# A graph-attention and mixture-of-experts kernel on one core: the middle of a step in another order, and a prologue that the planner orders

## The chip, the cores and the metric

The kernel runs on one core of a Trainium2 chip. A core has several engines, each of which works through its own list of instructions: TensorE (PE, matrix products; PEld in the tables is its loading of weights), VectorE (DVE), ScalarE (ACT), GpSimd (POOL) and SyncE (SP, which here only issues transfers). Engines wait for each other by semaphores. The metric is device time in microseconds (us) of one execution.

## The reference

There are 128 graphs of 64 nodes with 256 features each (8192 rows, float32), an adjacency matrix for each graph, and two layers. A layer is a graph attention over each graph's 64 nodes and then a mixture of experts in which each row takes the two best of eight experts; both are residual and both work on the layer norm of x.

```python
# layer 0 (layer 1 has a leaky ReLU on e, another gate, hidden 512, ReLU)
x = x + gnn(layernorm(x), adj)
x = x + ffn(layernorm(x))          # layer 0: ffn adds its tokens too

def gnn(h, adj):                   # h: 128 x 64 x 256
    Wh = h @ W
    e = (Wh @ a1)[:, :, None] + (Wh @ a2)[:, None, :]
    attention = softmax(where(adj > 0, e, -9e15), axis=-1)
    return elu(attention @ Wh)

def moe(tokens):                   # tokens: 8192 x 256
    logits = tokens @ router       # 8 experts
    w, e = top_k(logits, 2); w = softmax(w)
    return sum over both choices of w * (act(tokens @ w1[e] + b1[e]) @ w2[e] + b2[e])
```

Hidden size is 256 with GELU in layer 0 and 512 with ReLU in layer 1.

## The kernel before

**Blocks.** The rows of a layer are cut into 16 blocks of 512 rows (4 tiles of 128), so that there are 32 blocks in all. Each block has two Python generators, which are advanced stage by stage, so that the stages of several blocks can be woven together by hand.

`attend` (called through `a(i)`, one stage a call) does the attention of block i: layer-norm statistics on DVE, their reciprocal root on POOL (rs_g, L232) and the mask (cap_g, L279, POOL); the bias nb_g (L238, DVE) and the normalised xn_g (L240, ACT); the transposes pt_g on PE and their copies xt_g (L255 on DVE, L257 on ACT); the product pw_g with the weights (L290); sm_g (L301, DVE); the scores pe_g on PE (L309, L310) and ee_g, the masked exponentials; **a stage of two DVE instructions, the reciprocal of the sums and the normalising of ee_g (L334, L335)**; **a stage in which PE transposes ee_g into pp_g (L339) and pp_g is copied to pT_bd, one half by DVE (L341), the other by ACT (L342)**; the product po_g of pT_bd with wh_g (L348, PE) and its exponential ex_g (L356, ACT); and the sum xb_g (L362, L365, DVE).

`route` (called through `r(i)`) does the gating of block i: its layer norm (rs_r, nb_r, tn_r), the transposes pt_r, the logits pl_r (PE, L419) with the copy lg_r (L428) and a first search for the largest (L372 to L383, five DVE instructions); **the second search (L445 to L450: the best one masked, the five instructions again, and mm and q; eight small DVE instructions)**; the weights of the two choices; pn_r on PE (L476, L477), from which positions in the experts' lists follow (at_r, ps_r, ix_r, L479 to L494, DVE); eight indirect scatters of the rows into the lists in DRAM (L499, POOL); and a plan of which full groups of rows can be worked off.

**Slots.** Rows that are routed to one expert are worked off in slots of 256. SP fetches a slot's rows (xg_s, L688) and its expert's weights (wc_s, L740, L744, L748). Then `x()` transposes them (px_s on PE, L771, copy xT_s on DVE, L775), `h()` is the first product (ph_s, L853) with the activation on ACT (L862), and `y()` the second (py_s, L884) with the bias added on DVE (ys_s, L891). In layer 0 POOL scatters ys into res (L900); in layer 1 ACT weights it (L926) and POOL scatters it with accumulation into the output (L929).

**What sets the order.** The prologue starts three blocks' chains (and parts of blocks 3 and 4), woven by a list of calls (`chains`). Then the main loop runs one step for each t from FIRST = 3 to 31: it issues the attention of block n = t + 1, the routing of block t and t - 1 and the slots in an order written out by hand. `tc.manual_schedule(engines=ORDERED)`, entered before the first constant, holds four engines to the written order:

```python
ORDERED = {SP, mybir.EngineType.PE, mybir.EngineType.DVE, mybir.EngineType.Activation}
```

POOL is never held: a planner places its instructions, as it would on the other engines without this statement. The planner places by its own estimate of when operands are ready; each engine still runs what it was given in order. PSUM limits what can be in flight: the attention's tiles share two buffers (tag "a"), the routing's two (tag "r"), and px_s has one, ph_s two, py_s one.

Of the kernel before, what the change touches and what calls it, by code (L numbers as in the profile page):

```python
# [14 lines left out]
ORDERED = {SP, mybir.EngineType.PE, mybir.EngineType.DVE, mybir.EngineType.Activation}  # L15
# [20 lines left out]
def adj_ffn_kernel(  # L36
# [78 lines left out]
        return int(b >= CUT)  # L115

    ctx.enter_context(tc.manual_schedule(engines=ORDERED))
    ident = const.tile([P, P], F32, name="ident")  # L120
    make_identity(nc, ident)
    imod = const.tile([P, NG], F32, name="imod")
# [272 lines left out]
    def unordered(group, ins, keep=()):  # L395

        tc.declare_no_dep(
            ins.ins, group=group, keep=[i.ins for i in keep], reason="different rows"
        )
        tc.add_to_no_dep_group(group, ins.ins)  # L400
# [294 lines left out]
    class Slots:  # L695
# [140 lines left out]
        def h(self):  # L836
            k = self.nh
            self.weighted()
            if k == self.nx or k == self.ny + 2:
                return  # L840
            self.nh += 1
            sl = self.all[k]
            l = sl["l"]
            wc, xT = sl["wc"], sl["xT"]
            hT = slot.tile([P, HC[l], SL], F32, tag="hT", name=f"hT_s{k}")
            for f in range(0, HC[l], 2):
                ph = ps_s.tile([P, 2, SL], F32, tag="ph", name=f"ph_s{k}_{f}", bufs=2)
                cols = [slice(r.start * P, r.stop * P) for _, r in sl["of"]]
                for j in range(2):
                    for w, r in zip(wc, cols):  # L850
                        for c in range(KD):
                            o = c * HC[l] * P + (f + j) * P
                            nc.tensor.matmul(  # L853
                                ph[:, j, r],
                                lhsT=w[:, o : o + P],
                                rhs=xT[:, c, r],
                                start=(c == 0),
                                stop=(c == KD - 1),
                            )
                for j in range(2):  # L860
                    for w, r in zip(wc, cols):
                        nc.scalar.activation(  # L862
                            hT[:, f + j, r], ph[:, j, r], AF.Gelu if l == 0 else AF.Relu,
                            bias=w[:, OB1[l] + f + j : OB1[l] + f + j + 1],
                        )
            sl["hT"] = hT
            if l == 1 and sl["rest"]:
                self.spare(k)

        def y(self):  # L870
            k = self.ny
            self.weighted()
            if k == self.nh:
                return
            self.ny += 1
            sl = self.all[k]
            l = sl["l"]
            wc, hT = sl["wc"], sl["hT"]
            py = ps_s.tile([P, ST, D], F32, tag="py", name=f"py_s{k}")
            ys = slot.tile([P, ST, D], F32, tag="ys", name=f"ys_s{k}", bufs=4)  # L880
            for w, (_, r) in zip(wc, sl["of"]):
                for t in range(r.start, r.stop):
                    for f in range(HC[l]):
                        nc.tensor.matmul(  # L884
                            py[:, t, :],
                            lhsT=hT[:, f, t * P : (t + 1) * P],
                            rhs=w[:, O2[l] + f * D : O2[l] + (f + 1) * D],
                            start=(f == 0),
                            stop=(f == HC[l] - 1),
                        )  # L890
                nc.vector.tensor_tensor(  # L891
                    ys[:, r, :],
                    py[:, r, :],
                    w[:, OB2[l] : OB1[l]].unsqueeze(1).to_broadcast([P, r.stop - r.start, D]),
                    ALU.add,
                )
            sl["ys"] = ys
            for t in range(sl["st"]):
                if l == 0:
                    ins = nc.gpsimd.indirect_dma_start(  # L900
                        out=res[sl["part"]],
                        out_offset=self.row(sl, t),
                        in_=ys[:, t, :],
                        in_offset=None,
                        bounds_check=2 * N - 1,
                        oob_is_err=False,
                    )
                    unordered(f"res{sl['part']}", ins)
            if l == 1:
                self.ready = k  # L910
            self.ahead()
# [59 lines left out]
    def there(i):  # L971
        return 0 <= i < len(blks) and blks[i]

    def load(i, first=None):
        if there(i):
            k = blks[i]
            if k["l"]:
                assert all(s["l"] or s["part"] != part(k["b"]) for s in slots.all[slots.ny :])
            k["in"] = load_block(k["l"], k["b"], first)
            k["a"] = attend(k["l"], k["b"], k)  # L980

    def a(i, n=1):
        if there(i):
            for _ in range(n):
                next(blks[i]["a"], None)

    def r(i, n=1):
        if there(i):
            k = blks[i]
            if "r" not in k:  # L990
                k["r"] = route(k["l"], k["b"], k)
            for _ in range(n):
                next(k["r"], None)
# [49 lines left out]
    r(2, 2)  # L1043
    slots.fetch()
    slots.ahead()
    for t in range(FIRST, len(blks)):
        n = t + 1
        more = slots.nf - slots.ny > SB or len(slots.all) - slots.ny > SB
        if t + 3 != NB:
            load(t + 3)  # L1050
        a(n)
        h()
        x()
        a(n)
        r(t - 1)
        a(n)
        h()
        r(t)
        slots.fetch()
        if more:  # L1060
            x()
        a(n)
        r(t)
        early = n < len(blks) and blks[n]["l"] == 1
        if t + 2 != NB:
            a(t + 2)
        if early:
            a(n)
        y()
        r(t - 1)  # L1070
        if t + 2 != NB:
            a(t + 2)
        if not early:
            a(n)
        (h if more else x)()
        r(t)
        a(n)
        y()
        r(t - 1)
        a(t + 2, 1 + 2 * (t + 2 == NB))  # L1080
        if more:
            x()
        a(n)
        r(t)
        x()
        h()
        r(t - 1)
        a(n)
        if more:
            y()  # L1090
        x()
        r(t - 1)
        a(n)
        h()
        r(n)
        y()
        a(t + 2)
        r(t - 1)
        r(t)
        r(t)  # L1100
        y()
        slots.fetch()
        x()
        r(n)
        r(t)
        if t + 3 == NB:
            load(t + 3)
# [58 lines left out]
```

## Time and profile before

| what | value |
|---|---|
| median of 3 runs | 1396.14 us (1396.05 to 1398.04) |
| profiled execution | 1397.4 us, of which the span is 1395.6 us |
| instructions in the profile | 22284 |
| busy share of PE / PEld / DVE / ACT / POOL | 87% / 74% / 63% / 46% / 53% |
| mean granted clock of PE | 0.952 |
| matmuls of the slots, py_s L884 and ph_s L853 | 393.7 and 385.7 us |
| attention po_g L348 | 74.2 us busy, PE idle ahead of it 29.8 us |
| second half of pT_bd, L342 on ACT | 11.7 us busy |
| scatters of rows into the lists, L499 on POOL | 248.7 us, 256 instructions |
| scatters of ys, L929 and L900 on POOL | 213.0 and 144.5 us |
| first list fetch by SP, first px_s | 119.83 and 122.57 us after the span's start |

The profile shows one execution; times in it are microseconds from the span's start. A granted clock of 1.00 is PE's full speed. "Idle before, releaser" is the time in which an engine stood still just before an instruction and the event that ended the wait. A row of a list is one instruction or several equal ones in sequence, with the count at the end. The prologue lies in the first 120 us, the steps of layer 0 up to some 500 us, those of layer 1 up to some 1160 us, and the last slots after that.

### The profile page before, as it was taken

What the parts mean: (1) busy time and instruction counts of PE and PEld (TensorE: products, weight loads), DVE (VectorE), ACT (ScalarE), POOL (GpSimd) and SP (SyncE); (2) the same over time, 40 slices, a digit from 0 to 9 for tenths busy, and PEclk for the clock granted to TensorE, in tenths of its full rate; (3) what the DMA queues carried; (4) which work ended last, traced back from release to release, by engine and by line L of the source; (5) the groups of instructions that cost most, each with busy time, mean ns of one, the idle gap of its engine ahead of it and who ended that gap; (6) DMA issues with size and microseconds to landing.
All of it is one profiled execution on the core that took longest, in us unless ns stands there. A gap on an engine that the chain in (4) does not pass through costs nothing. (4 is left out here: it accounts for less than half of the span.)

```text
span 1395.6 us, 22284 instructions
## 1 busy us (share of the span) xinstructions
PE 1208.4 (87%) x6240; PEld 1035.8 (74%) x6240; DVE 872.5 (63%) x3390; ACT 647.2 (46%) x1550; POOL 742.3 (53%) x729
## 2 busy tenths in 40 slices
PE   6756799888889878888899999999999999998892
PEld 4545677777777767776788888888888887887881
DVE  3565677786677787776867666775667755432330
ACT  5533555655656544454544454444544443332320
POOL 3153666665566655465555655555655555533334
PEclk9767899999999999998999999999999999999996
DMA  7626467678776977867889888898888777698863
GB/s 208 181 80 198 160 210 258 208 244 254 233 237 224 307 252 245 276 219 236 265 274 276 238 238 210 233 269 223 249 217 222 208 203 208 189 280 248 247 167 39
DMA packets 262829, 311.69 MB, mean 223 GB/s; under 512 B 40615, under 2 KB 219950, under 8 KB 262704
## 3 DMA queue, kind: packets, MB, share of 16 engines
q1 hardware_dynamic: 219552, 225.02, 53.1%
q0 software_dynamic: 43152, 85.24, 22.9%
q8 instruction: 50, 0.82, 0.3%
q14 instruction: 75, 0.61, 0.2%
HBM read 212.25 MB, written 99.75 MB: 224 GB/s over the span
## 5 line engine op out<-in xcount | busy, mean ns | idle before, releaser
L884 PE MATMUL py_s<-wc_s,hT_s 128*128 128x256 f32 x1648 | 393.7, 388 | 39.9 <-issue 28.6
L853 PE MATMUL ph_s<-xT_s,wc_s 128*128 128x256 f32 (+1 forms) x1760 | 385.7, 371 | 19.3 <-DVE xT_s L775 8.5
L884 PEld LDWEIGHTS py_s<-wc_s,hT_s 128*128 128x128 f32 x1648 | 306.5, 192 | 88.9 <-issue 31.3
L853 PEld LDWEIGHTS ph_s<-xT_s,wc_s 128*128 128x128 f32 x1760 | 318.1, 193 | 65.3 <-DVE xT_s L775 14.5
L929 POOL DMA_INDIRECT out_dram<-ys_s,to_s x135 | 213.0, 1578 | 266.3 <-DMA out_dram<-ys_s,to_s 87.6
L499 POOL DMA_INDIRECT lists<-tn_r,ix_r x256 | 248.7, 971 | 108.3 <-issue 64.7
L862 ACT ACTIVATE hT_s<-ph_s,wc_s 128x256 f32<-128x256 f32 (+1 forms) x440 | 175.0, 457 | 145.0 <-PE ph_s L853 94.9
L900 POOL DMA_INDIRECT res<-ys_s,to_s x142 | 144.5, 1017 | 91.6 <-DVE ys_s L891 39.4
L891 DVE TENSOR_TENSOR ys_s<-py_s,wc_s 128x512 f32<-128x512 f32 (+1 forms) x149 | 97.1, 651 | 150.9 <-PE py_s L884 145.3
L775 DVE COPY xT_s<-px_s 128x512 f32<-128x512 f32 (+1 forms) x140 | 95.4, 682 | 87.4 <-PE px_s L771 87.3
L290 PE MATMUL pw_g<-gw,xt_g 128*128 128x258 f32 x512 | 125.8, 396 | 20.3 <-DVE xt_g L255 13.3
L290 PEld LDWEIGHTS pw_g<-gw,xt_g 128*128 128x128 f32 x512 | 96.7, 197 | 41.2 <-issue 13.2
L926 ACT ACTIVATE ys_s<-ys_s,cf_s 128x256 f32<-128x256 f32 x135 | 61.3, 499 | 102.6 <-DVE ys_s L891 102.4
L240 ACT ACTIVATE tn_r<-xb_g,nb_r,rs_r 128x256 f32<-128x256 f32 x128 | 66.4, 589 | 88.7 <-DVE nb_r L238 88.7
L240 ACT ACTIVATE xn_g<-xs,nb_g,rs_g 128x256 f32<-128x256 f32 x128 | 66.4, 589 | 81.3 <-DVE nb_g L238 81.3
L348 PE MATMUL po_g<-wh_g,pT_bd 128*128 128x256 f32 x256 | 74.2, 440 | 29.8 <-ACT pT_bd L342 28.3
L771 PE MATMUL px_s<-ident,xg_s 128*128 128x128 f32 x554 | 87.4, 281 | 5.7 <-DMA xg_s<-lists 3.2
L348 PEld LDWEIGHTS po_g<-wh_g,pT_bd 128*128 128x128 f32 x256 | 53.0, 217 | 47.1 <-ACT pT_bd L342 36.6
L771 PEld LDWEIGHTS px_s<-ident,xg_s 128*128 128x128 f32 x554 | 71.7, 148 | 19.7 <-DMA xg_s<-lists 3.5
L279 POOL TENSOR_SCALAR cap_g<-adj 128x256 f32<-128x256 int32 x32 | 35.3, 1104 | 81.3 <-DMA adj<-in_adj_dram 56.7
L297 ACT COPY wh_g<-pw_g 128x258 f32<-128x258 f32 x128 | 47.9, 375 | 59.1 <-PE pw_g L290 58.5
L342 ACT COPY pT_bd<-pp_g 64x256 f32<-64x256 f32 x32 | 11.7, 364 | 129.4 <-DVE pT_bd L341 129.3
(503 smaller groups left out, 1620.0 us busy)
## 6 DMA issues: line engine op xcount, KB each, us to landing
wc_s<-in_w_dram SPq DMA_DIRECT2D x142, 512.0 KB, 5.3
wc_s<-in_w_dram SPq DMA_DIRECT2D x156, 256.0 KB, 4.0
xg_s<-lists SPq DMA_DIRECT2D x64, 260.0 KB, 4.3
xg_s<-lists SPq DMA_DIRECT2D x64, 258.0 KB, 3.6
yb<-res SPq DMA_DIRECT2D x16, 1024.0 KB, 10.4
wc_s<-bcat SPq DMA_DIRECT2D x78, 129.0 KB, 4.0
wc_s<-bcat SPq DMA_DIRECT2D x71, 130.0 KB, 4.9
xs<-in_x_dram SPq DMA_DIRECT2D x16, 512.0 KB, 4.2
```

The lines of the kernel that those rows point to most:

```text
L240: nc.scalar.activation(outs(t), xb[:, t, :], AF.Identity, bias=nb[:, t : t + 1], scale=rs[:, t : t + 1])
L290: nc.tensor.matmul(pw, lhsT=xt[:, k, t * P : (t + 1) * P], rhs=gw[l][:, k, :], start=(k == 0), stop=(k == KD - 1),)
L348: nc.tensor.matmul(po[h][:, j, :], lhsT=pT[:, 2 * h + j, :], rhs=wh[:, 2 * h + j, 0:D], start=True, stop=True,)
L499: ins = nc.gpsimd.indirect_dma_start(out=lists[l], out_offset=bass.IndirectOffsetOnAxis(ap=ix[:, k, t : t + 1], axis=0), in_=tn[:, t, 0 : ...
L771: nc.tensor.transpose(px[:, c, t * P : (t + 1) * P], xg[:, t, c * P : (c + 1) * P], ident)
L775: nc.vector.tensor_copy(xT[:, :, 0 : st * P], px[:, :, 0 : st * P])
L853: nc.tensor.matmul(ph[:, j, r], lhsT=w[:, o : o + P], rhs=xT[:, c, r], start=(c == 0), stop=(c == KD - 1),)
L862: nc.scalar.activation(hT[:, f + j, r], ph[:, j, r], AF.Gelu if l == 0 else AF.Relu, bias=w[:, OB1[l] + f + j : OB1[l] + f + j + 1],)
L884: nc.tensor.matmul(py[:, t, :], lhsT=hT[:, f, t * P : (t + 1) * P], rhs=w[:, O2[l] + f * D : O2[l] + (f + 1) * D], start=(f == 0), stop=(f ...
L891: nc.vector.tensor_tensor(ys[:, r, :], py[:, r, :], w[:, OB2[l] : OB1[l]].unsqueeze(1).to_broadcast([P, r.stop - r.start, D]), ALU.add,)
L900: ins = nc.gpsimd.indirect_dma_start(out=res[sl["part"]], out_offset=self.row(sl, t), in_=ys[:, t, :], in_offset=None, bounds_check=2 * N - 1,
L929: ins = nc.gpsimd.indirect_dma_start(out=out, out_offset=self.row(sl, t), in_=ys[:, t, :], in_offset=None, compute_op=ALU.add,)
```

## The change

Two things are moved; nothing is added or left out, and the numbers of instructions on each engine stay the same.

The statement that holds the engines to the written order is entered just ahead of the main loop, after the prologue's last call. So SP, PE, DVE and ACT get the planner's order in the prologue, and the written order in the main loop.

In the middle of a step, two calls of `a(n)` are moved. The stage that normalises ee_g (for blocks of layer 0; in layer 1 it stood earlier already) goes ahead of a `y()`, an `r(t - 1)` and an `a(t + 2)`. The stage with pp_g and pT_bd goes ahead of `r(t)`, which is the second search, so that the second search comes last.

```diff
@@ -115,8 +115,6 @@
         return int(b >= CUT)
 
 
-
-    ctx.enter_context(tc.manual_schedule(engines=ORDERED))
     ident = const.tile([P, P], F32, name="ident")
     make_identity(nc, ident)
     imod = const.tile([P, NG], F32, name="imod")
@@ -1043,6 +1041,8 @@
     r(2, 2)
     slots.fetch()
     slots.ahead()
+
+    ctx.enter_context(tc.manual_schedule(engines=ORDERED))
     for t in range(FIRST, len(blks)):
         n = t + 1
         more = slots.nf - slots.ny > SB or len(slots.all) - slots.ny > SB
@@ -1066,15 +1066,15 @@
             a(t + 2)
         if early:
             a(n)
+        if not early:
+            a(n)
         y()
         r(t - 1)
         if t + 2 != NB:
             a(t + 2)
-        if not early:
-            a(n)
         (h if more else x)()
+        a(n)
         r(t)
-        a(n)
         y()
         r(t - 1)
         a(t + 2, 1 + 2 * (t + 2 == NB))
```

In the built program the orders of PE, ACT and SP in the main loop are those of before. On DVE the copy pT_bd (L341) stands ahead of the eight instructions of the second search in every step, and in the steps of layer 0 L334 and L335 stand ahead of the first ys (L891). On POOL, rs_g (L232) stands behind the first output scatter of the same slot for one slot in each of nine steps of layer 1. In the prologue all engines have another order. The lines of the changed file's body are two lower than those of the kernel before (L341 is L339 there).

## The prediction

> **What bounds the kernel now.** I read the page's first part, then a table of windows, then PE's waits and the lists of instructions in order of time (start, duration, engine, line, operation, tile, count; in brackets the idle time just before and what ended it).
>
> ```profile
> span 1395.6 us, 22284 instructions
> PE 1208.4 (87%) x6240; PEld 1035.8 (74%) x6240; DVE 872.5 (63%) x3390; ACT 647.2 (46%) x1550; POOL 742.3 (53%) x729
> ```
> ```profile
> 80.00:100.00 20.00, 13.78 (x57) 10.94 (x55) 12.66 (x69) 10.04 (x27) 12.39 (x13) 0.57 0.27 93
> 100.00:120.00 20.00, 7.36 (x26) 5.91 (x27) 9.66 (x51) 4.39 (x10) 13.91 (x15) 0.66 0.26 93
> 760.00:1110.00 350.00, 331.72 (x1719) 287.57 (x1718) 234.95 (x911) 160.73 (x413) 198.00 (x160) 1.00 0.84 232
> ```
>
> The columns are the stretch, its length, busy PE, PEld, DVE, ACT, POOL, granted clock, DMA share and GB/s. In the steps of layer 1 PE is busy 331.7 of 350 us: only PE's waits can be won there. From 100 to 120, before the first slots, PE has 7.4 busy us of 20, and POOL is the fuller engine. So one half of the change meets a PE-bound loop, the other a prologue bound by a chain of dependences.
>
> The waits of PE from 760 to 1110, then the place of one of the first row's nine:
>
> ```profile
> PE po_g L348 <- ACT pT_bd L342: 12.1, 9, 1.4
> PE py_s L884 <- issue: 3.7, 8, 0.5
> PE pp_g L339 <- DVE ee_g L335: 1.6, 6, 0.3
> ```
> ```profile
> 930.65 3.72 PE L884 MATMUL py_s<-wc_s,hT_s 128*128 128x256 f32 x16
> 933.35 0.18 DVE L445 SCALAR_TENSOR_TENSOR l_r<-oh_r_9a,lg_r 128x32 f32<-128x32 f32 x1
> ...
> 934.79 0.15 DVE L450 TENSOR_TENSOR q_r<-mx_r_9b,mx_r_9a 128x4 f32<-128x4 f32 x1
> 934.87 0.41 DVE L341 COPY pT_bd<-pp_g 64x256 f32<-64x256 f32 x1
> 935.20 0.67 DVE L891 TENSOR_TENSOR ys_s<-py_s,wc_s 128x512 f32<-128x512 f32 x1
> 935.31 0.36 ACT L342 COPY pT_bd<-pp_g 64x256 f32<-64x256 f32 x1 [7.85 <-DVE pT_bd L341]
> 935.73 1.56 PE L348 MATMUL po_g<-wh_g,pT_bd 128*128 128x256 f32 x6 [1.35 <-ACT pT_bd L342]
> ```
>
> The eight operations of the second search (L445 to L450) take DVE 1.52 us, and pT_bd stands behind them though pp_g was done at 930.74. ACT copies its half after DVE's, then PE starts po_g.
>
> The prologue:
>
> ```profile
> 85.10 0.17 DVE L494 CAST ix_r<-pos_r 128x8 int32<-128x8 f32 x1
> 85.57 1.10 POOL L499 DMA_INDIRECT lists<-tn_r,ix_r  x1 [4.17 <-DVE ix_r L494]
> 106.63 1.06 POOL L232 TENSOR_TENSOR rs_r<-ve_r,nhalf 128x4 f32<-128x4 f32 x1
> 107.88 1.03 POOL L499 DMA_INDIRECT lists<-tn_r,ix_r  x1 [0.19 <-DVE nb_r L238]
> 112.59 6.15 PE L290 MATMUL pw_g<-gw,xt_g 128*128 128x258 f32 x16 [13.00 <-DVE xt_g L255]
> 119.83 3.08 SPq L688 DMA_DIRECT2D xg_s<-lists  x4
> ```
>
> Once ix_r of block 0 is there, POOL issues 24 scatters, 1.27 us apart, to 117.77; then SP fetches the first lists and px_s starts at 122.57. The first slots are bound by ix_r0 plus this chain; the 13.00 us of PE hang on the same chain (xt_g of block 4 stands behind nb_r, which waits for POOL's rs_r).
>
> **Layer 1, n = 22 to 30 (nine steps).** The order on PE, ACT and SP is unchanged in the loop; on DVE pT_bd goes ahead of the eight. pT_bd then starts at 933.35, ACT's half at 933.79 to 934.15, and PE could start some 0.06 later, at 934.21. The py_s ahead of it ends at 934.38. So the whole wait goes: 9 x 1.35 = 12.1. The search costs nothing where it stands: the ys behind both starts at 935.20 as before, and DVE then has 4.53 us idle (at 948.56, for py_s of PE). The next limit is xT_s before ph_s at 954.42, whose wait is 0.07. On POOL, which the written order does not hold, rs_g moves behind a scatter of ys in these steps (slots 77, 81 ... 109). It starts at 939.40 now, would start near 945.5 and end by 947.2. Its reader nb_g stands at 949.16, 1.35 earlier then: about 0.7 us is left. If this cover goes, nb_g and the xn_g, xt_g behind it are late, at most until the 1.35 is gone. Ends 0 and 12.1; I take 12.1, since the row itself shows all that is behind the wait.
>
> **Other layer 1 steps.** n = 16: po_g waits 2.81 (523.74), of which the search is 1.52; DVE idles 1.38 just after (527.85), so 1.4. n = 17: po_g waits 2.98, but DVE has no gap from 548 to 577: 0. n = 20: 1.64, but DVE's slack is 0.22: 0.2. At n = 18, 19, 21, 31 other waits end last: 0. Together 1.6; ends 0 and 1.52 x 3 = 4.6.
>
> **Layer 0, n = 6 to 10 and 15.** Here L334 and L335 (0.17 + 0.42) also go ahead of the first ys. In one such step (240 to 276):
>
> ```profile
> 247.03 0.69 DVE L891 TENSOR_TENSOR ys_s<-py_s,wc_s 128x512 f32<-128x512 f32 x1 [0.44 <-DMA lists<-tn_r,ix_r]
> 248.41 0.60 PE L339 MATMUL pp_g<-ident,ee_g 128*64 128x128 f32 x4 [0.98 <-DVE ee_g L335]
> 251.29 1.99 PE L348 MATMUL po_g<-wh_g,pT_bd 128*128 128x256 f32 x8 [0.55 <-ACT pT_bd L342]
> ```
>
> PE waits 0.98 + 0.55 = 1.53, but only DVE's 0.44 to 0.52 idle before ys can be filled: from there to xT_s at 263.94 DVE never stops, and PE's ph_s waits for that xT_s (0.55). What PE wins beyond that comes back there as a longer wait. Six steps, 2.9 in all; ends 0 and 9.2. The ys, up to 0.2 later, delays its res scatter on POOL, which no PE wait names. n = 11 to 14 hold no such idle time: 0.
>
> n = 4: po_g waits 1.85 (127.41) behind the search's 1.52, and DVE idles 2.42 at 131.71: 1.95 with the pp_g wait's part, ends 0 and 3.15 (both waits). n = 5: DVE idles 0.52 and 0.67: 1.2; its px_s waits for a fetch, so the low end is 0.
>
> **The prologue.** Without the written order the planner mixes the chains; counts do not change. What moves, on every queue: on PE, pn_r of block 0 (before 79.82) goes ahead of the second layer's make_gw and of pw_g of block 3; on DVE the second search of block 0 comes early, but BN statistics of blocks 1 and 2 go ahead of nb_g of block 0 (some 2.4 us at the start); on ACT, pT_bd of block 0 no longer stands behind four xn_g; on SP the 16 pad writes (13.77 us from 46.32) come earlier and the load of block 6 is now in the prologue. Carrying the rows' durations through the new orders: po_g of block 0 near 30.5 (32.37 before), pl_r0 near 47 (51.93), pw_g of block 3 done near 69.5, sm_g behind it near 71 (77.48), and ix_r0, which stands just behind that sm_g, near 73: 12.3 earlier than 85.3. Two losses: cap_g of block 6 (1.1, L279) now lies inside POOL's chain, 1.2; and ix_r2 stands behind nb_r of block 3, which waits for rs_r between the scatters, 2.4. So -12.3 + 1.2 + 2.4 = -8.7. Ends: -15 (ix_r0 held by pn_r0 near 62 alone, 5.4 from there to ix_r0 as from 79.82 to 85.27: 67.4, so -17.9 + 3.6, rounded up) and +3.6 (ix_r0 no earlier, both losses paid). This is an estimate carried through forty orders, the weakest term.
>
> PE would then idle some 10 us ahead of px_s. The trace has a row for that: after its 13.00 us idle the 16 pw_g took 6.15 where others take 3.83, and po_g 3.78 against 1.99, at a window clock of 0.66. [...]
>
> **Sum.** -8.7 - 1.95 - 1.2 - 2.9 - 1.6 - 12.1 = -28.4. The profiled execution took 1397.4 (span 1395.6 and 1.8 around it): 1369.0. It lies 1.3 above the median of the runs, 1396.14; so 1368.
>
> **Rivals.**
> 1. The prologue gives nothing: ix_r0 comes earlier, but some link later (ix_r2, nb_r of block 3) holds the first fetch. For it: the chain has some dozen links in a new order. Against: 13 us of idle PE and 8.53 of DVE (before 73.92) that a better order can use. 1397.4 - 19.7, less 1.3: 1376.
> 2. The loop's gain comes back: rs_g behind a scatter on POOL, or the weights (DMA share 0.84) arriving later than PE now asks. For it: only 0.7 us are left at nb_g. Against: PE's wait rows from 760 to 1110 name no DMA. With the prologue's 8.7 and a third of the loop: 1397.4 - 8.7 - 6.6, less 1.3: 1381.
> 3. More than I count: the layer 0 waits go whole (9.2) and ix_r0 lands near 67 (-15): 1397.4 - 15 - 3.15 - 1.2 - 9.2 - 1.6 - 12.1, less 1.3: 1354.
> 4. Slower: cap_g of block 6 stands on POOL between the scatters of block 0 and block 1 and waits for the adj load of block 6, behind an xs load whose buffer is free only after xb_g of block 2 (L362, 60.54 now). With 4.1 us for the load that is near 70; POOL reaches it near 84. If adj came after 112 (84 + 8.7 + 19.7), the kernel would be slower; at 120, by 8: 1404. The 14 us of slack speak against.
> 5. The change does nothing: the planner returns to the written order. The built order excludes it for DVE's middle; the prologue alone is rival 1.
>
> **How the numbers follow.** Main 0.52, rival 1 0.20, rival 2 0.13, rival 3 0.06, rival 4 (and other stalls of an order nobody wrote) 0.09. The predicted time is the main case's. Its own range is 1362 to 1375. The range over the cases leaves out rival 4 and part of rival 3 and of 2: 1357 to 1386. Faster by over 0.2% (2.8 us, about what these runs can tell from no change): 0.88; within it, the weak end of rivals 2 and 4: 0.03; slower: 0.09.
>
> **What would show it.** In the changed profile: between 760 and 1110 no po_g wait for pT_bd of over 0.3, and a step of 41.7 in place of 43.06 us; pT_bd ahead of L445's operation (L443 then); DVE's idle before the ys near 948 still over 2 us. First px_s near 114 (122.57) and ix_r0 near 73. In layer 0, the pp_g wait gone and ph_s's wait for xT_s grown to about 1.6. Wrong if nb_g waits for POOL's rs_g in layer 1, if the 12.1 shows up as waits for wc_s, or if the first px_s lies at or behind 122.

## The result, and the profile after

The changed kernel takes 1359.47 us (median of 4 runs, 1357.05 to 1365.68), the kernel before 1396.51 us on the same chip (4 runs, 1396.05 to 1398.04). The ratio is 0.974, with a 95% interval of 0.971 to 0.977. Forecast were 1368 us and a range of 1357 to 1386. The profiled execution of the changed kernel is its slowest, 1365.68 us, with a span of 1363.8 us. So sums over its trace show less gain than the median: 31.8 us of span against 37.0 us. In four of the experiments below (e9, e10, e12 and e13) every kernel, the one before included, took some 18% longer, with PE standing still ahead of pw_g (in e9 17 times, up to 9.7 us) for a reason that stays open, so that their times are compared with each other alone.

The first part of the page and the table of windows of the changed kernel (columns as before: stretch, length, busy PE, PEld, DVE, ACT, POOL, clock, DMA share, GB/s):

```profile
span 1363.8 us, 22282 instructions
PE 1194.0 (88%) x6240; PEld 1027.1 (75%) x6240; DVE 864.3 (63%) x3390; ACT 645.5 (47%) x1550; POOL 745.0 (55%) x729
```
```profile
80.00:100.00 20.00, 12.30 (x39) 8.74 (x38) 9.59 (x52) 4.83 (x11) 14.63 (x15) 0.52 0.30 106
100.00:120.00 20.00, 12.47 (x59) 10.49 (x60) 10.85 (x38) 7.75 (x20) 5.03 (x6) 0.74 0.70 221
760.00:1110.00 350.00, 344.58 (x1801) 300.76 (x1800) 241.53 (x939) 167.02 (x434) 209.29 (x169) 1.00 0.82 237
```

In the steps of layer 1 PE is now busy 344.6 of 350 us (331.7 before). The stretch from 100 to 120 already holds the first slots.

PE's waits in the nine steps of layer 1, and the middle of the step that the prediction showed:

```profile
PE py_s L882 <- issue: 3.7, 8, 0.5
PE pp_g L337 <- DVE ee_g L333: 0.6, 3, 0.2
```
```profile
900.05 3.72 PE L882 MATMUL py_s<-wc_s,hT_s 128*128 128x256 f32 x16
902.89 0.41 DVE L339 COPY pT_bd<-pp_g 64x256 f32<-64x256 f32 x1
903.22 0.17 DVE L443 SCALAR_TENSOR_TENSOR l_r<-oh_r_9a,lg_r 128x32 f32<-128x32 f32 x1
903.33 0.36 ACT L340 COPY pT_bd<-pp_g 64x256 f32<-64x256 f32 x1 [6.33 <-DVE pT_bd L339]
903.75 2.00 PE L346 MATMUL po_g<-wh_g,pT_bd 128*128 128x256 f32 x8
...
904.73 0.69 DVE L889 TENSOR_TENSOR ys_s<-py_s,wc_s 128x512 f32<-128x512 f32 x1
915.72 1.63 POOL L230 TENSOR_TENSOR rs_g<-ve_g,nhalf 128x4 f32<-128x4 f32 x1
917.39 0.16 DVE L236 SCALAR_TENSOR_TENSOR nb_g<-mv_g,rs_g 128x4 f32<-128x4 f32 x1
...
959.52 0.16 DVE L236 SCALAR_TENSOR_TENSOR nb_g<-mv_g,rs_g 128x4 f32<-128x4 f32 x1 [0.86 <-POOL rs_g L230]
```

The row "po_g <- pT_bd, 12.1 us, 9 times" is gone; py_s runs into po_g without a gap. The step takes 41.4 us (po_g at 903.75 and 945.14) in place of 43.06. The last three lines show that the cover on POOL is gone: rs_g ends at 917.35 and nb_g starts 0.04 later, on a DVE that had been idle since 917.27; in the next step nb_g waits 0.86 us for rs_g. In four of the nine steps (blocks 27 to 30) DVE stood so for 0.12, 0.86, 0.29 and 0.20 us. No loss of PE by it shows: each of the nine steps won 1.5 to 1.7 us at po_g.

The prologue:

```profile
68.35 1.10 POOL L497 DMA_INDIRECT lists<-tn_r,ix_r  x1 [4.30 <-DVE ix_r L492]
78.42 1.08 POOL L277 TENSOR_SCALAR cap_g<-adj 128x256 f32<-128x256 int32 x1
91.44 1.06 POOL L230 TENSOR_TENSOR rs_r<-ve_r,nhalf 128x4 f32<-128x4 f32 x1
94.19 1.02 POOL L497 DMA_INDIRECT lists<-tn_r,ix_r  x1 [1.70 <-DVE ns_p L546]
105.86 4.42 SPq L686 DMA_DIRECT2D xg_s<-lists  x4
109.28 1.12 PE L769 MATMUL px_s<-ident,xg_s 128*128 128x128 f32 x4 [6.62 <-DMA xg_s<-lists]
```

The first scatter comes 17.2 us earlier (85.57 before), the first px_s 13.3 us earlier (122.57).

I set each PE instruction's start against that of the same instruction before. The difference grows like this (stretches end at the first px_s and then at a py_s of the slots; the last column is the forecast):

| stretch | won, us | forecast, us |
|---|---|---|
| prologue, to the first px_s | 13.3 | 8.7 |
| n = 4, to the first py_s (120.31) | 1.8 | 1.95 |
| n = 5, to py_s 167.50 | 1.7 | 1.2 |
| n = 6 to 15, to py_s 494.46 | 3.1 | 2.9 |
| n = 16, to py_s 527.71 | 1.6 | 1.4 |
| n = 17 to 21, to py_s 729.37 | 2.9 | 0.2 |
| n = 22 to 30, to py_s 1078.48 | 14.1 | 12.1 |
| last slots | -6.7 | 0 |
| sum, in span | 31.8 | 28.4 |

### The profile page after: what moved, and what is told of

The parts are those of the page before. It is cut to its first block, busy times and chain, and to the rows that moved or that the text cites. A ratio compares the mean times of both kernels' runs of the same rounds, so it can differ in the third digit from the quotient of the medians.

```text
span 1363.8 us, 22282 instructions
## 1 busy us (share of the span) xinstructions
PE 1194.0 (88%) x6240; PEld 1027.1 (75%) x6240; DVE 864.3 (63%) x3390; ACT 645.5 (47%) x1550; POOL 745.0 (55%) x729
## 3 DMA queue, kind: packets, MB, share of 16 engines
q0 software_dynamic: 43152, 85.24, 22.8%
## 5 line engine op out<-in xcount | busy, mean ns | idle before, releaser
L288 PE MATMUL pw_g<-gw,xt_g 128*128 128x258 f32 x512 | 129.2, 403 | 14.5 <-ACT wh_g L295 6.2
L346 PE MATMUL po_g<-wh_g,pT_bd 128*128 128x256 f32 x256 | 68.3, 412 | 7.9 <-ACT pT_bd L340 7.0
L230 POOL TENSOR_TENSOR rs_r<-ve_r,nhalf 128x4 f32<-128x4 f32 x32 | 39.3, 1229 | 54.2 <-DVE ve_r L228 51.1
L417 PEld LDWEIGHTS pl_r<-rw,xt_r 128*128 128x128 f32 x512 | 63.8, 196 | 6.4 <-ACT xt_r L255 4.3
L346 PEld LDWEIGHTS po_g<-wh_g,pT_bd 128*128 128x128 f32 x256 | 49.7, 202 | 21.0 <-ACT pT_bd L340 10.5
```

What stands on the lines that cost most here:

```text
L288: nc.tensor.matmul(pw, lhsT=xt[:, k, t * P : (t + 1) * P], rhs=gw[l][:, k, :], start=(k == 0), stop=(k == KD - 1),)
L346: nc.tensor.matmul(po[h][:, j, :], lhsT=pT[:, 2 * h + j, :], rhs=wh[:, 2 * h + j, 0:D], start=True, stop=True,)
```

## The experiments

**Each half alone, and each move undone.** These four ran on one chip, where the kernel before took 1394.25 us (10 runs). Diffs are against the changed kernel, but for e2.

e1, the loop alone: the statement stands at its old place, the step is the changed one.

```diff
+    ctx.enter_context(tc.manual_schedule(engines=ORDERED))
     ident = const.tile([P, P], F32, name="ident")
...
-    ctx.enter_context(tc.manual_schedule(engines=ORDERED))
     for t in range(FIRST, len(blks)):
```

> Only the middle of the step is changed; the prologue keeps the written order. Theory A (the two parts add up): the profile of the changed kernel shows 13.3 us won by the first px_s and 25.2 more up to the last block's po_g, of which the last slots gave back up to 6.7. So this kernel keeps px_s at 122.6, wins 22 to 25 us after it, and takes about 1373 us; the step of layer 1 takes 41.4 us. Theory B (part of the loop's gain came from the other start, by clock windows that fell otherwise): the gain is only the forecast's 19.7 or less, 1377 us or more.

Measured: 1375.35 us (1373.38 to 1378.71), ratio 0.984 (0.981 to 0.988); first px_s at 122.33; 20.2 us won by the last po_g. The time lies between the theories, the trace gives nearly theory B's number. The 5 us that the changed kernel wins more between px_s and the last po_g do not come from another order in the loop, which is the same in both kernels on every engine but for one cap_g on POOL at its start. 3.3 us of it arise at one place, around the ph_s ahead of po_g of n = 7. These windows begin at the same work, first of this kernel, then of the changed one:

```profile
200.00:210.00 10.00, 8.11 (x33) 6.63 (x34) 5.38 (x23) 4.50 (x10) 7.76 (x8) 0.83 1.02 344
```
```profile
185.00:195.00 10.00, 9.29 (x50) 7.78 (x49) 6.91 (x29) 5.83 (x14) 7.66 (x8) 1.00 1.03 351
```

Two things differ. Up to the start of that ph_s this kernel falls back by 1.8 us: PE waits 1.89 us there against 0.71, for a DVE that had itself stood 0.93 us until POOL, busy with a scatter, had done rs_g; in the changed kernel DVE doesn't wait there. Then the granted clock of the window is 0.83 in this kernel and 1.00 in the changed one; there the other 1.5 us arise, and 33 matmuls lie in the window in place of 50. So a part of the gain, of some 3 us, lies at a wait on POOL and in a stretch with a lower granted clock, which one execution has and the other has not.

e2, the prologue alone: the statement at its new place, the step as before (the diff is against the kernel before).

```diff
-    ctx.enter_context(tc.manual_schedule(engines=ORDERED))
     ident = const.tile([P, P], F32, name="ident")
...
+    ctx.enter_context(tc.manual_schedule(engines=ORDERED))
     for t in range(FIRST, len(blks)):
```

> Only the prologue is left to the planner; the step's middle is as before. Theory A (adds up): px_s starts near 109.3, nothing more is won behind it, about 1383 us, and the step of layer 1 stays at 43.06 us. Theory B (an earlier start is eaten by the loop, for instance by the transfers of the first blocks): 1390 us or more.

Measured: 1386.30 us (7 runs, 1380.42 to 1390.01), ratio 0.993 (0.989 to 0.996). The first px_s is at 110.87, and the shift stays between 12.6 and 13.5 us from n = 5 to n = 20 and ends at 11.5: the loop keeps it. po_g waits 12.1 us, 9 times, in layer 1 as before. Theory A for the mechanism; of the median, 3 us are missing, and the seven runs scatter over 9.6 us. With the loop's 20.2 this makes 31.7 us by the last po_g, against 38.5 of both together.

e3, the first move undone (pT_bd stays ahead of the search):

```diff
-        if not early:
-            a(n)
         y()
         r(t - 1)
         if t + 2 != NB:
             a(t + 2)
+        if not early:
+            a(n)
```

> The changed kernel with one part undone: in layer 0 the normalising stage (L332, L333) stands behind the first ys again; pT_bd stays ahead of the second search. Theory A (the first move is worth the 0.5 us of DVE idle time that it fills in each of six steps of layer 0): pp_g waits about 1 us again in layer 0, 2 to 3 us are lost, about 1362 us. Theory B (what PE wins at pp_g comes back in full at py_s, since DVE is the bound there): no loss, 1359 us.

Measured: 1371.39 us (1368.53 to 1372.88), ratio 0.981 (0.978 to 0.985). Both theories fall: the move is worth far more, 7.8 us by the trace, all of it before n = 16. From 130 to 490 us pp_g waits for the normalised ee_g as in the kernel before (7.7 us in 6 waits there, 0.2 in the changed kernel):

```profile
PE pp_g L337 <- DVE ee_g L333: 8.9, 7, 2.6
```

Without the first move, pT_bd ahead of the search even loses against the kernel before in layer 0: the shift at po_g goes from 16.1 us (n = 4) to 13.3 us (n = 15). Some 1 us of this is lost at n = 10, where the granted clock was 0.83 from 290 to 300 us, and 1.00 over the same work before. For n = 11 to 14 the trace shows what is new. DVE in this kernel at n = 12:

```profile
367.76 0.42 DVE L333 TENSOR_TENSOR ee_g<-ee_g,erc_g 128x256 f32<-128x256 f32 x1
369.11 0.42 DVE L339 COPY pT_bd<-pp_g 64x256 f32<-64x256 f32 x1 [0.93 <-PE pp_g L337]
369.45 0.17 DVE L443 SCALAR_TENSOR_TENSOR l_r<-oh_r_11a,lg_r 128x32 f32<-128x32 f32 x1
```

DVE comes to pT_bd before PE has made pp_g, and stands. Before, the eight instructions of the search filled that time. The changed kernel has the same wait in the same four steps, n = 11 to 14 (from 120 to 500 us):

```profile
DVE pT_bd L339 <- PE pp_g L337: 5.4, 4, 1.5
```

e4, the other move undone (the search ahead of pT_bd again):

```diff
         (h if more else x)()
-        a(n)
         r(t)
+        a(n)
         y()
```

> The changed kernel with the other part undone: the second search stands ahead of pT_bd again in all steps. Theory A (pT_bd behind the search is what PE waits for in layer 1): po_g waits 1.35 us again in nine steps, the step of layer 1 takes 43.0 us, and with n = 16 to 21 and some of layer 0 about 16 us are lost, 1375 us. Theory B (the other engines' limits are close, so the order matters less): 8 us or less are lost, below 1368 us.

Measured: 1378.04 us (1376.55 to 1383.52), ratio 0.988 (0.983 to 0.992). Theory A: 15.7 us are lost by the last po_g, 14.4 of them in n = 22 to 30, where the wait is back:

```profile
PE po_g L346 <- ACT pT_bd L340: 12.1, 9, 1.4
```

In layer 0 nothing is lost: from n = 4 to n = 15 this kernel wins 7.6 us on the kernel before, the changed one 6.1. Step by step, the changed kernel gains 1.1 us on this one up to n = 10, loses 3.8 at n = 11 to 14, the steps with DVE's wait for pp_g, and gains 1.2 at n = 15.

**What in the prologue's order brings the gain.** e5 to e8 ran on another chip, where the kernel before took 1392.08 us. The changed kernel with PE (e5), DVE (e6) or both (e12) held to the written order in the prologue, one run of each; the diff is that of e5:

```diff
+    prologue = ExitStack()
+    prologue.enter_context(tc.manual_schedule(engines={mybir.EngineType.PE}))
...
+    prologue.close()
     ctx.enter_context(tc.manual_schedule(engines=ORDERED))
```

> The changed kernel, but in the prologue PE alone is held to the written order (SP, DVE and ACT are the planner's). Theory A (the prologue's gain comes from PE's order: pn_r of block 0 no longer stands behind the second layer's weight products, pw_g of block 3 and its pe_g): with PE's order back, ix_r0 is at 80 us or later and the first px_s at 119 or later, most of the 13.3 us is lost. Theory B (the gain comes from DVE's order, which puts block 0's search and statistics early): ix_r0 stays below 72 and px_s below 113.

> The changed kernel, but in the prologue DVE alone is held to the written order. Theory A (PE's order is what counts): ix_r0 stays below 74 and the first px_s below 115. Theory B (DVE's order is what counts): ix_r0 is at 80 or later and px_s at 119 or later. If both this run and the one with PE held lose most of the gain, the two orders only help together.

> The changed kernel, but in the prologue PE and DVE are both held to the written order; ACT, SP and POOL are the planner's. With PE alone held the first px_s was at 113.4, with DVE alone at 114.8. Theory A (the two orders are the gain, each a part): px_s at 118 or later. Theory B (ACT's and SP's orders carry most of it): px_s still below 116.

The first px_s of the three, in this order:

```profile
113.41 1.12 PE L771 MATMUL px_s<-ident,xg_s 128*128 128x128 f32 x4 [6.14 <-DMA xg_s<-lists]
```
```profile
114.82 1.11 PE L771 MATMUL px_s<-ident,xg_s 128*128 128x128 f32 x4 [8.89 <-DMA xg_s<-lists]
```
```profile
120.58 1.12 PE L771 MATMUL px_s<-ident,xg_s 128*128 128x128 f32 x4 [7.79 <-DMA xg_s<-lists]
```

The times were 1367.22 and 1371.90 us and, for e12, 1611.97 (the kernel before 1654.78). The first scatter came at 75.04, 77.68 and 82.07. Against the 109.28 of the changed kernel, PE's order costs 4.1 us of 13.3 when it is put back, DVE's 5.5, both 11.3, nearly all. Eight executions with the planner's prologue left as it is (the changed kernel twice, e2, e3, e4, e8, e10, e13; the order is the same on every engine up to the first slots) had px_s at 107.1 to 110.9, so that the single costs are uncertain by almost their own size; that both orders together are most of the gain is clear of this. Theories A and B of the single runs both fall, that of the two orders as parts stands.

**What bounds layer 0.** e7, pT_bd in layer 0 copied by ACT alone:

```diff
-        nc.vector.tensor_copy(pT[0:NG, :, 0:NG], pp[:, :, 0:NG])
+        if l == 0:
+            nc.scalar.copy(pT[0:NG, :, 0:NG], pp[:, :, 0:NG])
+        else:
+            nc.vector.tensor_copy(pT[0:NG, :, 0:NG], pp[:, :, 0:NG])
```

> The changed kernel with one copy moved: in layer 0 both halves of pT_bd are copied by ACT, so that DVE has 0.41 us less to do in each block and never waits for pp_g. Theory A (DVE bounds the steps of layer 0, and its new wait for pp_g, 5.4 us in all, is lost there): 0.4 us for each of 12 steps and some 2 us at n = 11 to 14 are won, about 1353 us. Theory B (PE's own waits for hT_s on ACT and for transfers bound these steps): within 2 us of 1359.

Measured: 1360.91 us (1357.01 to 1367.78), ratio 0.975 (0.969 to 0.980), not told apart from the changed kernel. The trace says more. Against the changed kernel's it wins 1.4 us at n = 12 and 1.1 at n = 13, where DVE's waits for pp_g are gone, but only 0.1 at n = 11, where one is gone too. It wins 1.5 at n = 10, where po_g no longer waits 1.04 us for pT_bd, 0.4 and 0.3 at n = 8 and 9, nothing at n = 6 and 7. It loses 1.2 at n = 16, in the matmuls behind a wait of 3.93 us that both kernels have (ph_s and py_s took 2.52 and 3.10 us there in the changed kernel, 1.89 each elsewhere), starts 2.4 later from the prologue and loses 2.8 more behind the last po_g. So the wait for pp_g is in part a cost that can be taken away, and it is too small to be seen in these medians. Theory A is right for some of the steps from n = 8 to 13 and wrong as a rule for every step.

e8, the search ahead of pT_bd for n = 11 to 14 alone:

```diff
-        a(n)
+        rest = 11 <= n <= 14
+        if not rest:
+            a(n)
         r(t)
+        if rest:
+            a(n)
```

> The changed kernel, but for n = 11 to 14 (the steps with slots of two experts) the second search stands ahead of pT_bd again. Theory A (there DVE comes to pT_bd before pp_g is done, waits 1 to 1.5 us, and the search had filled that time): the two steps that lost 1.1 us each win them back, about 1357 us. Theory B (the loss at n = 11 and 12 has another cause): no change, 1359.5 us.

Measured: 1363.46 us (1354.42 to 1364.23), ratio 0.975 (0.969 to 0.982): no change. In the trace the step to po_g of n = 12 is 1.15 us shorter, as theory A has it; the one to n = 11 is not, so that its loss of 1.1 us has another cause, which stays open; and that to n = 13 loses 1.26 again. Between n = 12 and 13 the granted clock was lower, 0.66 against 0.83 over 10 us, and the four py_s behind a wait of 1.86 us took 2.08 us against 1.13; this kernel, then the changed one, over the same work:

```profile
375.00:385.00 10.00, 8.03 (x28) 6.71 (x29) 4.62 (x25) 4.62 (x9) 7.67 (x9) 0.66 0.81 243
```
```profile
377.00:387.00 10.00, 7.04 (x31) 5.96 (x32) 5.57 (x27) 4.62 (x10) 7.53 (x8) 0.83 0.74 216
```

**The changed kernel once more, and the search first in layer 0.** e9 is the changed kernel itself.

> The changed kernel itself once more, to see what differs between two executions of one program. Theory A (executions differ by which of PE's waits fall into the half-rate records of its clock, by the start of the prologue, and by how long the last accumulating scatters take to land): the order of all engines being the same, the first px_s lies within 2 us of 109.3, the shift against the kernel before between px_s and the last po_g within 3 us of 25.2, and the last scatters make up the rest. Theory B (the gain of the profiled execution is the same to within 0.5 us in each stretch): then what the other runs show beyond their edits is caused by these edits.

Measured (e9): ratio 0.969 (0.965 to 0.973) to the kernel before (1654.78 us). The first px_s is at 107.11, 2.2 us earlier with the same program: just outside the 2 us of theory A and far outside the 0.5 of theory B. The later stretches can't be set against the first trace, so that the rest of theory A was not tested.

The same with the search first in layer 0, twice (e10, e13):

```diff
-        a(n)
+        if early:
+            a(n)
         r(t)
+        if not early:
+            a(n)
         y()
```

> The changed kernel, but in layer 0 the second search stands ahead of pT_bd again (in layer 1 behind it). Theory A (in layer 0 the search is a cover for DVE's wait for pp_g, and DVE, not po_g, bounds these steps): nothing is lost in layer 0, from the first py_s to n = 15 it is 0 to 2 us ahead of the changed kernel, and the steps of layer 1 keep 41.4 us: 1357 to 1360 us. Theory B (pT_bd ahead of the search is worth its 0.55 us in layer 0 as well): 3 us or more are lost before n = 15, 1362 us or more.

> The kernel with the second search ahead of pT_bd in layer 0 and behind it in layer 1, once more, since the chip of the last set took 18% longer for every kernel and PE stood still there for reasons that its profile does not show. Theory A (in layer 0 DVE is the bound and the search covers its wait for pp_g): no wait of DVE for pp_g over 2 us in all between 120 and 500, from the first py_s to n = 15 this kernel wins as much as the changed one (6.1 us from po_g to po_g) or up to 2 us more, the step of layer 1 is 41.4 us, the time 1357 to 1361 us or 0.972 to 0.976 of before. Theory B: 3 us or more are lost between n = 4 and n = 15, 1362 us or more.

Measured: ratio 0.968 (0.963 to 0.973) and 0.973 (0.968 to 0.977). DVE's wait for pp_g falls from 7.1 us in all (the changed kernel in e9) to 1.5 and 0.9, which lie in the prologue alone. From po_g of n = 4 to that of n = 15 the two runs took 460.3 and 457.3 us against 463.0 of the changed kernel in e9: nothing is seen to be lost in layer 0 by the search standing first, theory A, though two executions of one program differ by 3 us here. By the whole time the two orders are not told apart. No version here beats the changed kernel beyond its interval.

## Why the prediction was right, and where it was off

The time lies in the stated range, and 8.5 us below the 1368 forecast; the main case's own range of 1362 to 1375 was missed by 2.5 us. The profiled executions, of which the sum was made, moved by 31.8 us against 28.4. This closeness is in part luck: 4.6 us more in the prologue, 2.7 more at n = 17 to 21 and 2.0 more at n = 22 to 30 stand against 6.7 lost in the last slots.

**Layer 1, n = 22 to 30: right.** The whole wait went, nothing took its place; e4 brings back the very row. It was 14.1 us in place of 12.1, and 41.4 us a step in place of 41.7; 1.0 us of the difference is pp_g's wait, which fell from 1.6 us over the stretch to 0.6, the rest is not laid to a row. DVE's idle time ahead of the ys (3.10 at 916.58, 4.53 before) covers the search, as said. The cover on POOL was wrong: of the 0.7 us that were to be left, nothing was left in four of the nine steps. nb_g waits for POOL's rs_g there, up to 0.86 us, which the prediction had named as a sign of being wrong and as the condition of rival 2. That the gain stayed even so, with 1.5 to 1.7 us in each of these steps too, means that xn_g and what follows it had slack behind nb_g, which the prediction had not counted on.

**Prologue: right in kind, a term mis-sized.** "ix_r0 near 73" measured 68, so 17.2 us and not 12.3. The links: pn_r of block 0 at 58.47 (forecast near 62), pw_g of block 3 done at 66.2 (69.5), sm_g at 67.00 (71), ix_r0 at 67.88. I had carried the durations of the rows of before, several of them from stretches with a granted clock of 0.53 (50 to 60 and 65 to 70 us; in the changed kernel it was 0.85 from 55.0 to 66.2); that this is the whole of the difference was not worked out. It is near the low end's 67.4 and rival 3's 67, but the other half of rival 3, 9.2 us in layer 0, did not come. The two losses were well sized: the way from the first scatter to the first of block 1 grew from 11.12 to 12.39 us (1.27 for cap_g, forecast 1.2), and to the first of block 2 from 22.31 to 25.84 (2.26 more for ix_r2 behind nb_r, forecast 2.4). The first px_s is 13.3 us earlier and e2 shows that the loop keeps it, so rivals 1 and 4 are out.

**Layer 0: the sum right, some of its steps wrong.** It was 3.1 us against 2.9. For n = 7 to 10 the account held: po_g won 0.6, 0.6, 0.7 and 1.0 us step by step, near the 0.44 to 0.52 that DVE had idle, and the waits at pp_g and po_g, 1.53 together, were gone. But they came back at another place: ph_s's wait for xT_s grew only from 0.55 to 0.8, where the prediction said 1.6, and most of it stands at py_s behind ys. The first row is of the kernel before, the others are of the changed one:

```profile
260.16 1.97 PE L884 MATMUL py_s<-wc_s,hT_s 128*128 128x256 f32 x8 [0.47 <-issue]
```
```profile
239.53 0.39 PE L475 MATMUL pn_r<-mm_r,ones 128*128 128x32 f32 x2
241.46 0.89 PE L882 MATMUL py_s<-wc_s,hT_s 128*128 128x256 f32 x3 [1.54 <-issue]
```

The gap is 1.07 more, of the 1.53 won at pp_g and po_g; DVE works without a gap of over 0.1 from 227.13 to 242.11, with the statistics of the block ahead of the ys that frees py_s (it ends 0.1 ahead of py_s in both kernels). "n = 11 to 14: 0" was wrong: from po_g of n = 10 to that of n = 14 the changed kernel lost 2.3 us, and at n = 15 it won 2.2. What I did not see is DVE's wait for pp_g at pT_bd, 5.4 us in these four steps; without it e8 wins 1.15 us at n = 12 and e7 1.4 and 1.1 at n = 12 and 13, while the loss at n = 11 stays. I had also credited the two moves together: e3 and e4 show that the first alone is worth 7.6 to 7.8 us (some 1 us of the latter at the granted clock of 0.83 in e3), and that pT_bd ahead of the search loses 1.5 to 3 in layer 0.

**n = 17 to 21: forecast 0.2, won 2.9.** Not by a wait of the sum. In the kernel before, the granted clock around n = 19 was 0.50 from 636.7 to 643.1 us, in the first of these windows, and the four py_s there took 2.08 us against 1.13 in the changed kernel; the second is the same work in the changed kernel, the third in e4:

```profile
635.00:645.00 10.00, 7.85 (x25) 6.52 (x26) 6.63 (x24) 2.94 (x5) 4.76 (x5) 0.66 0.67 218
```
```profile
613.00:623.00 10.00, 7.12 (x37) 6.13 (x37) 7.52 (x28) 4.96 (x9) 5.51 (x6) 1.00 0.77 238
```
```profile
615.00:625.00 10.00, 7.78 (x43) 6.95 (x44) 7.60 (x26) 5.06 (x8) 4.84 (x6) 1.00 0.69 221
```

The wait at py_s in these windows was 3.04 us before and 2.88 in the changed kernel, but e4 has the 3.04 too, with a granted clock of 1.00. So the gain doesn't need the shorter wait; what set the clock was not shown. No term of the forecast stands for it, and as far as the forecast goes it was luck.

**The clock at the first slots: rightly left out.** The sum of the forecast counts nothing for it. px_s did start slower (1.12 us in place of 0.66), and the granted clock was 0.50 from there to 116.2, 6.9 us; but before it was 0.50 from 124.3 to 131.1 too, 6.8 us (the 3.78 us of po_g lie there), and n = 4 still won 1.8 of the forecast 1.95.

**The last slots: missed.** The forecast had no term there, and the profiled execution lost 6.7 us: 3.7 up to the end of PE's last product, 3.0 behind it. Its chain that ended last, near the end:

```profile
1310.84 5.44 DMA out_dram<-ys_s,to_s
1317.07 3.71 DMA out_dram<-ys_s,to_s
1321.53 3.80 DMA out_dram<-ys_s,to_s
...
1332.41 1.55 POOL out_dram L927
1334.26 3.86 DMA out_dram<-ys_s,to_s
1338.90 1.55 POOL out_dram L927
1340.76 3.80 DMA out_dram<-ys_s,to_s
```

From 1310 on, 53 us ahead of the end, the time goes mostly by accumulating scatters (their landing is 56.9% of the chain from 1308 on), which wait 2.9 to 4.7 us, mostly in pairs, for the landing of those before; in the kernel before that began at 1364, 31 us ahead of the end, behind products of PE:

```profile
1357.60 3.47 PE py_s L884 x16
...
1364.21 1.55 POOL out_dram L929
```

Waits for weights grew as well (ph_s for wc_s: 6.4 us before, 7.9 after). The other runs show that this end takes back more where more was won ahead of it: e2, with 11.5 us won by the last po_g, won 3.4 more behind it; e1 and e4, with 20.2 and 22.8, lost 1.5 and 3.8; and the five others with over 30 (e3 and e5 to e8) lost 2.6 to 9.6. So a part of what is won in the loop doesn't reach the end, as rival 2 had it, though for the most part not by its two causes. Why the scatters took over earlier wasn't tried. The median won 37.0 us; where it lost less than the profiled execution isn't shown.

## What to carry to other kernels

A copy that is put ahead of independent work wins only where its operand is ready: where the engine comes to it early, the work that stood ahead was a cover, and the wait turns up on that engine instead of on its consumer (DVE's 5.4 us here). Undo each move of a change by itself, since two moves can add up to the forecast with one worth double and the other less than nothing, as they did in layer 0. And where a hand-written order covers only the steady state, leaving the start-up to the planner can be worth as much as a tuned wait in nine steps (13.3 and 14.1 us here).

## What was unexpected of the hardware

PE's granted clock differed from execution to execution over the same work: 0.66 against 1.00 (n = 19, with a wait of 3.04 us in both the kernel before and e4), 0.83 against 1.00 (e1 and the changed kernel, whose loops have one order but for a cap_g on POOL) and 0.66 against 0.83 (e8 and the changed kernel). Beside the lower clock stood 1.5 us lost in e1 and 1.26 in e8, and beside the higher one 2.7 us won over the forecast at n = 17 to 21. What set the clock was not shown. A change worth less than some 3 us in this kernel can be read from its wait rows, and not from the time of an execution.
